# Layer 0 of a four-layer convolution kernel: group norm by half batches, a second channel tile taken from resident buffers, part of the statistics on ScalarE, another order of memory pools

## The chip, the cores and the metric

The kernel runs on one core of a Trainium2 chip. The core has five engines that run their own instruction streams and wait for one another by semaphores: TensorE (PE in the profile; PEld is its weight load), VectorE (DVE), ScalarE (ACT), GpSimd (POOL) and SyncE (SP). Transfers are issued from the queues of SP, ACT and POOL. The metric is the device time of one execution in microseconds (us). Three runs of the kernel before took 3128.01, 3133.1 and 3138.59 us, median 3133.1.

## The reference

The input `x` has shape (8, 384, 32, 32): eight images, 384 channels. Four layers follow one another, each `x = x + layer(group_norm(x))` with 32 groups of 12 channels. Layer 0 is the one that the change touches:

```python
def _bn(x, g, b):                       # mean and variance over all 8 images and all pixels
    m = x.mean(axis=(0, 2, 3), keepdims=True)
    v = x.var(axis=(0, 2, 3), keepdims=True)
    return (x - m) * lax.rsqrt(v + EPS) * g[None, :, None, None] + b[None, :, None, None]

def _dwproj(x, dw, g, b, pw):
    C = x.shape[1]
    y = lax.conv_general_dilated(x, dw, (1, 1), ((1, 1), (1, 1)), feature_group_count=C, ...)
    y = jax.nn.gelu(_bn(y, g, b), approximate=False)
    return jnp.einsum('oc,bchw->bohw', pw, y)

q = _dwproj(x, dw_q, g_q, b_q, pw_q).reshape(B, heads, hd, N)
k = _dwproj(x, dw_k, g_k, b_k, pw_k).reshape(B, heads, hd, N)
v = _dwproj(x, dw_v, g_v, b_v, pw_v).reshape(B, heads, hd, N)
attn = jax.nn.softmax(jnp.einsum('bhcn,bhcm->bhnm', q, k) * scale, axis=-1)
out = jnp.einsum('bhnm,bhcm->bhcn', attn, v).reshape(B, C, H, W)
out = jnp.einsum('oc,bchw->bohw', w_out, out)
return _bn(out, g_out, b_out)

def _gn(v, G=32, eps=1e-5):             # mean and variance of one image and one group
    g = v.reshape(B_, G, C_ // G, H_, W_)
    m = jnp.mean(g, axis=(2, 3, 4), keepdims=True)
    s = jnp.var(g, axis=(2, 3, 4), keepdims=True)
    return ((g - m) / jnp.sqrt(s + eps)).reshape(v.shape)
```

Two kinds of statistics matter. The group norm's are of one image each, so that four images can be normed before the other four are seen. The batch norm's (`_bn`) after each 3x3 depthwise convolution are of all eight images, so that the Gelu and the projections of q, k and v need all eight images of that convolution. Layers 1 to 3 (a mixture of experts, a 7x7 depthwise convolution, a branched mixer) come later in time and are not changed.

## The kernel before

The 384 channels lie as three channel tiles (`ct` 0 to 2) of 128 partitions; `VORDER = (1, 0, 2)` is the order k, q, v.

**Opening.** SP loads channel tiles 0 and 1 of all eight images into `x0` and `x1`. These two are the two buffers of the tag `o` in pool `co`; later the same buffers take the convolution's output. For each image and tile VectorE takes statistics (`x_stats`: two BATCH_NORM_STATS2 and an aggregate, L252 and L437). Then `gn_steps` (L259 to L300) norms all eight images of two channel tiles at once: TensorE averages over groups with small matmuls against `gmatA` (L279), VectorE forms centred moments (L290 to L293), TensorE averages these, VectorE adds epsilon (L246), POOL raises to the power -0.5 (`rsqrt`, L247), VectorE forms the offset (L297). `prepare0(0, b)` then applies scale and offset on ScalarE (`affine`, L354) and transposes 32x32 blocks on VectorE (L468) into `xt0`, which the convolution reads. Three parameter tensors (`bn_gb`, `bn_gbo`, `b2`) are loaded through ScalarE's queue.

**The loop.** The convolution runs as matmuls with banded weights. There are 36 groups, `groups = [(ct, v, u) ...]`: three channel tiles, three convolutions, four quarters `u` of the columns; four groups make one (ct, v). A group is 96 matmuls (L530) into one of two PSUM slots `ps`. Its other steps, in program order:

- `spread0(n + 2)` makes the matmul weights `wx` from loaded weights `w`, half on ScalarE (L486) and half on POOL (L487).
- `weights_of(n + 3)` issues the load of a later group's weights on ScalarE's queue (L478), three buffers.
- In groups 0 and 1, `stats2(b)` loads and measures channel tile 2 of four images each. After group 1 the norm of all three tiles and eight images begins, in a PSUM slot of its own between the groups (`slot0`); after group 2 it ends.
- `prepare0(1, b)` after groups 3, 4, 8, 9 and 10 loads channel tile 1 of each image again into a buffer `xn` (three buffers), norms and transposes it. `prepare0(2, b)` does the same for tile 2 in groups 12, 13, 16, 17 and 20.
- `results(ct, v, b, o)` for the four groups before: VectorE transposes an image's output back (L501), takes its batch norm statistics (L252, into `stats`), and SP stores it to `raw` (L503). The images go 1, 2, 2, 3 over the four groups; the last (ct, v) has its eight images after the loop.
- `evict_slots` copies the PSUM slot to `o` on ScalarE (L405). There are two `o` buffers: the first eviction of four groups needs the results of two sets before to be done.
- `coefs0(v)` turns the statistics of a finished convolution into a scale and an offset: three aggregates (L364), then L246, L247 and L367 to L369. It comes in groups 31 and 35 and after the loop. `gelu0` activates image 0 of k in groups 32 to 34, of q after the loop.

**After the loop.** `attention` loads `pw_v`, `w_out` (pool `aw`) and v of image 0 (`y`, pool `ay`) through SP, projects k and q of image 0 (L671), activates v and projects it (L726), and then runs attention image by image.

**What sets the order.** Within layer 0 the order on TensorE, ScalarE, VectorE and POOL is the order of the program text (`manual_schedule`); each engine takes its instructions strictly in order. SP's order, and POOL's in `attention`, is chosen by a planner. Pools lie on one stack of memory in the order in which they are opened: `cw` (statistics and parameters), `cxa` (`xt0`), `cy`, `co`. When they close, the pools of `attention` lie over the same addresses from the bottom, and what is written there waits for the last reader of what lay there. A DMA that is issued on SP's or ScalarE's queue can also wait for an earlier, unrelated DMA.

Of the kernel before, what the change touches and what calls it, by code (L numbers as in the profile page):

```python
# [18 lines left out]
P = 128  # L19
# [156 lines left out]
def conv_mixer_kernel(ctx: ExitStack, tc: tile.TileContext, a: dict, out: bass.AP):  # L176
# [82 lines left out]
    def gn_steps(mv, pool_ps, tag="gn", order="A"):  # L259
# [25 lines left out]
        def new(name):  # L285
            return small.tile(shape, FP, tag=f"gn_{name}{shape[1:]}", name=f"gn_{name}")
# [9 lines left out]
        rsqrt(flat(s), flat(pv))  # L296
        nc.vector.scalar_tensor_tensor(  # L297
# [114 lines left out]
    with (  # L412
        tc.tile_pool(name="cw", bufs=1) as cw,
        tc.tile_pool(name="cxa", bufs=1) as cxa,
        tc.tile_pool(name="cy", bufs=3, reuse_waits="tile") as cy,
        tc.tile_pool(name="co", bufs=2, reuse_waits="tile") as co,
        tc.manual_schedule(engines=ORDERED | {mybir.EngineType.Pool}),
    ):
        bn_gb = load(cw, "bn_gb", nc.scalar)
        bn_gbo, b2s = (load(cw, k, nc.scalar) for k in ("bn_gbo", "b2"))  # L420
# [7 lines left out]
        stats = cw.tile([P, 9, 2 * B, 6], FP, name="stats")  # L428

# [9 lines left out]

        with tc.tile_pool(name="cgn", bufs=2, space=PSUM) as cgn:  # L440
            pm = cgn.tile([P, NC, 2], FP, tag="gmy", name="pm", bufs=1)
            over_groups(pm, consts, range(NC))
            nc.scalar.copy(gmy, pm)
            for b in range(B):
                nc.sync.dma_start(out=x0[:, b], in_=a["x"][b, :, 0])
                nc.sync.dma_start(out=x1[:, b], in_=a["x"][b, :, 1])
                x_stats(0, b, x0[:, b])
                x_stats(1, b, x1[:, b])
            norms = {0: gn_coefs((mvx[:, 0, :2], mvx[:, 1, :2]), cgn)}

        with tc.tile_pool(name="cps", bufs=2, space=PSUM, reuse_waits="tile") as cps:
            xt0s = {}

            def prepare0(ct, b):

                if b == 0:
                    pool = cxb if ct == 1 else cxa
                    xt0s[ct] = pool.tile([P, 32, B, H + 2], FP, tag="xt0", name="xt0")
                    for row in (0, H + 1):
                        nc.gpsimd.memset(xt0s[ct][:, :, :, row : row + 1], 0.0)  # L460
                if ct == 0:
                    xn = x0[:, b]
                else:
                    xn = cy.tile([P, N], FP, tag="xn", name="xn")
                    nc.sync.dma_start(out=xn, in_=a["x"][b, :, ct, :])
                sx, tx = norms[ct]
                affine(xn, xn, sx[:, ct, b : b + 1], tx[:, ct, b : b + 1])
                nc.vector.transpose(  # L468
                    xt0s[ct][:, :, b, 1 : 1 + H].rearrange("p c h -> p h c"), img(xn)
                )  # L470

            groups = [(ct, v, u) for ct in range(NC) for v in VORDER for u in range(4)]
            weights0 = {}

            def weights_of(n):
                if n < len(groups):
                    w = cy.tile([P, 24, W], FP, tag="w", name="w")
                    nc.scalar.dma_start(out=w, in_=a["w0"][groups[n]])  # L478
                    weights0[n] = w

            def spread0(n):

                if n < len(groups):
                    w = weights0[n]
                    x = weights0[n] = cy.tile([P, 24, 2, W], FP, tag="wx", name="wx")
                    nc.scalar.activation(x[:, :, 0, :], w, AF.Copy, scale=parity[:, 0:1])  # L486
                    nc.gpsimd.tensor_scalar(x[:, :, 1, :], w, parity[:, 1:2], None, ALU.mult)  # L487

            def slot0():

                ps = cps.tile([P, 4, 2, B, H], FP, tag="ps", name="ps")
# [2080 lines left out]
```

## Time and profile before

| What | us |
|---|---|
| Median of three runs | 3133.1 |
| The profiled execution's own time | 3131.1 |
| Its span, first to last instruction | 3129.4 |
| First convolution matmul (L530) | 52.83 |
| First transposed result (L501) | 95.55 |
| Last convolution matmul ends | 274.2 |
| Last statistics of the last result end | 302.4 |
| First matmul on `pw_v` (L726) | 316.87 |
| Mean ACTIVATE of 128x1024 (L354, tile `y`) | 1.23 |
| Mean eviction of 128x2048 (L405, loop) | 1.86 |
| Power on POOL: 128x3, 128x16, 128x24 elements | 0.87, 2.94, 4.20 |

All times of the profile are of one execution, counted from its first instruction. A line of a timeline gives the start, the duration, the engine, the line of the kernel, the operation, what it writes and reads, how many instructions were merged, and in brackets the idle time of that engine before it with the releaser. A line of the stage table gives the length of the stage, each engine's busy time in it with the number of instructions, the granted clock of TensorE as a share of full speed, the busy share of the DMA engines and what they moved. A line of the waits gives the waiting engine and line, the one waited for, the total, the number of waits and the longest.

### The profile page before, as it was taken

The page shows a single profiled execution, that of the slowest core. Times are in us where ns is not written, and L with a number is a line of the kernel's source. Part 1 is how long each engine was busy: PE and PEld are TensorE (multiplying, and loading weights), DVE is VectorE, ACT ScalarE, POOL GpSimd, SP SyncE. Part 2 cuts the span into 40 slices and gives each one's busy share as a digit, 9 for nine tenths or more (in the row PEclk, how much of TensorE's full clock was granted, in tenths as well). Part 3 has the DMA queues.
Part 4 walks back from the last instruction along what each step waited for, and adds up shares of the span by engine and source line. Part 5 has one row for each costly group of instructions (what it writes and reads, how often), then busy time and mean ns, then how long its engine had stood idle before and what let it go on. Part 6 is the DMA issues. An engine that isn't in the chain of part 4 may idle for free. (4 is left out here: it accounts for less than half of the span.)

```text
span 3129.4 us, 45250 instructions
## 1 busy us (share of the span) xinstructions
PE 2978.0 (95%) x18280; PEld 1710.8 (55%) x18280; DVE 1857.4 (59%) x3066; ACT 1211.5 (39%) x1446; POOL 858.7 (27%) x1103
## 2 busy tenths in 40 slices
PE   4988999999999999999999999999999999886998
PEld 3765334343433434343433688788787877555543
DVE  6898344445454445444445777777777776457164
ACT  2655453544445353545433122222222223446520
POOL 2432000000000000000000577686777764111400
PEclk9999999999999999999999999999999999898999
DMA  6787102010111101110002111112112114967675
GB/s 220 262 281 287 57 23 83 23 63 23 61 46 41 63 23 63 44 63 23 31 23 94 74 41 65 57 49 85 45 45 81 52 37 161 335 204 251 232 227 187
DMA packets 89107, 323.03 MB, mean 103 GB/s; under 512 B 13608, under 2 KB 16000, under 8 KB 84664
## 3 DMA queue, kind: packets, MB, share of 16 engines
q1 hardware_dynamic: 64936, 251.71, 23.6%
q10 hardware_dynamic: 13776, 35.82, 3.7%
q0 software_dynamic: 10176, 32.51, 3.0%
q8 instruction: 146, 2.39, 0.3%
q14 instruction: 73, 0.60, 0.1%
HBM read 211.66 MB, written 111.68 MB: 103 GB/s over the span
## 5 line engine op out<-in xcount | busy, mean ns | idle before, releaser
L780 ACT ACTIVATE e<-sc 128x1024 f32<-128x1024 f32 x512 | 483.2, 1031 | 607.8 <-PE sc L773 607.7
L773 PE MATMUL sc<-qT,kT 64*128 64x512 f32 x2048 | 473.9, 602 | 0.0
L792 PE MATMUL av<-e,vT 128*64 128x512 f32 x2048 | 467.7, 599 | 0.0
L773 PEld LDWEIGHTS sc<-qT,kT 64*128 64x128 f32 x2048 | 186.8, 186 | 282.0 <-issue 231.3
L792 PEld LDWEIGHTS av<-e,vT 128*64 128x64 f32 x2048 | 135.5, 136 | 316.4 <-issue 316.4
L822 POOL DMA_DIRECT2D att<-att x45 | 23.7, 531 | 979.6 <-DVE att L817 979.6
L671 PE MATMUL sc<-y,pw 128*128 128x512 f32 x576 | 249.3, 594 | 0.0
L808 DVE LOAD_MASK_SELECT sm<-av x64 | 0.9, 14 | 417.0 <-PE av L792 417.0
L530 PE MATMUL ps<-xt,wx 64*64 64x256 f32 x3456 | 198.7, 388 | 35.2 <-DVE xt L468 20.1
L810 DVE RECIPROCAL inv<-sm 128x512 f32<-128x512 f32 x64 | 214.6, 3353 | 2.2
L1346 POOL TENSOR_TENSOR hs_sum<-hs,hs_sum 128x256 f32<-128x256 f32 (+1 forms) x225 | 209.7, 940 | 9.4
L1366 DVE TENSOR_TENSOR r<-r,p 128x256 f32<-128x256 f32 x416 | 153.2, 411 | 92.2 <-PE p L1357 90.7
L530 PEld LDWEIGHTS ps<-xt,wx 64*64 64x64 f32 x3456 | 156.8, 137 | 76.1 <-issue 39.7
L671 PEld LDWEIGHTS sc<-y,pw 128*128 128x128 f32 x576 | 108.8, 190 | 139.9 <-issue 138.5
L354 ACT ACTIVATE hs<-hs,b 128x512 f32<-128x512 f32 x135 | 88.4, 712 | 247.4 <-DVE hs L1308 246.8
L1116 PE MATMUL ps<-xt,wx 64*64 64x256 f32 (+1 forms) x2912 | 160.5, 379 | 23.8 <-ACT wx L1725 12.8
L1357 PE MATMUL p<-hs_sum,wsum 128*128 128x256 f32 x768 | 177.0, 384 | 0.0
L1308 DVE TENSOR_TENSOR hs<-p,hs_sum 128x256 f32<-128x256 f32 x270 | 114.5, 424 | 93.5 <-PE p L1299 39.0
L1299 PE MATMUL p<-forms,w 128*128 128x256 f32 x630 | 165.4, 379 | 0.0
L1323 PE MATMUL ph<-xn,w 128*128 128x512 f32 x342 | 159.3, 600 | 3.0 <-ACT xn L354 3.0
L1357 PEld LDWEIGHTS p<-hs_sum,wsum 128*128 128x128 f32 x768 | 149.2, 194 | 21.4
L1116 PEld LDWEIGHTS ps<-xt,wx 64*64 64x64 f32 x2912 | 109.2, 139 | 73.3 <-ACT wx L1725 15.1
(346 smaller groups left out, 4687.3 us busy)
## 6 DMA issues: line engine op xcount, KB each, us to landing
raw<-y SPq DMA_DIRECT2D x72, 512.0 KB
y<-raw SPq DMA_DIRECT2D x24, 1536.0 KB
x<-x SPq DMA_DIRECT2D x23, 608.0 KB
xt<-x SPq DMA_DIRECT2D x23, 608.0 KB
w<-in_w ACTq DMA_DIRECT2D x36, 384.0 KB
xn<-in_x SPq DMA_DIRECT2D x24, 512.0 KB
x<-in_x SPq DMA_DIRECT2D x16, 768.0 KB
z<-z POOLq DMA_DIRECT2D x16, 768.0 KB, 4.3
```

What stands on the lines that cost most here:

```text
L530: nc.tensor.matmul(ps[64 * d : 64 * d + 64, 2 * i + e, cc], lhsT=w[r, 12 * cc + 6 * e + 3 * d + k, :], rhs=xt0s[ct][r, 16 * d + 4 * u + 2 ...
L671: nc.tensor.matmul(ps[:, h, :], lhsT=w[:, ct, pair, :], rhs=y[:, ct, h * HF : (h + 1) * HF], start=ct == 0, stop=ct == NC - 1,)
L773: nc.tensor.matmul(sc[:, s, :], lhsT=kTs[b][r, pair, m * P : (m + 1) * P], rhs=qTs[b][r, pair, h * HF : (h + 1) * HF], start=True, stop=True,)
L780: nc.scalar.activation(e, sc, AF.Exp, scale=1.0 if shifted else HD**-0.5)
L792: nc.tensor.matmul(av[64 * s : 64 * s + 64, :], lhsT=vTs[0][:, m, c0 : c0 + 64], rhs=e[:, s, :], start=m == 0, stop=m == N // P - 1,)
L810: nc.vector.reciprocal(inv, sm)
L1116: nc.tensor.matmul(ps[64 * d : 64 * d + 64, 2 * i + e, c % 2, images], lhsT=w[r, d * K7 + k, :], rhs=by_slot(xts[ct])[r, 16 * d + column(c ...
L1299: nc.tensor.matmul(ps[:, :QF], lhsT=block1(PRODUCTS[n][0])[:, e], rhs=form_of(n, xn), start=True, stop=True,)
L1323: nc.tensor.matmul(ph, lhsT=w1[:, e, ct, dc * P : (dc + 1) * P], rhs=xn[:, ct, :], start=ct == 0, stop=ct == NC - 1,)
L1346: eng.tensor_add(rows_of(o, hs, s), rows_of(i, hs, s), rows_of(j, hs, s))
L1357: nc.tensor.matmul(ps[:, :QF], lhsT=block(w)[:, e], rhs=rows_of(x, hs, e), start=e == 0, stop=e == E - 1,)
L1366: nc.vector.tensor_tensor(out=o, in0=o, in1=ps[:, :QF], op=op)
```

## The change

1. **Opening.** The norm of tiles 0 and 1 is made in two halves of four images (`norm_steps`; `gn_steps` gets a pause before its last step, and tiles in pool `cw`). The first half's steps stand between the statistics of images 4 to 7; the second half's between the first transposes of `prepare0(0, b)`. The weights of groups 0 and 1 are loaded on SP's queue after image 3, and spread there; those of group 2 on ScalarE's queue later. The averaging of the constants (`pm`, `gmy`) moves behind the transposes. The three parameter loads go from ScalarE's queue to POOL's.
2. **Norm in the loop.** Also by halves. Each half's two passes over groups are put into the second halves of the PSUM slots of groups 2 and 3, between or ahead of these groups' own matmuls. `stats2` of images 4 to 7 is spread over groups 1 and 2. All eight images of tile 1 are prepared by group 4, in place from `x1`, with no second load.
3. **Statistics.** Of images 2 and 4, in all but the last (ct, v), VectorE takes no statistics. ScalarE makes two passes (`scalar_sums`, Identity and Square with an accumulated sum, against the channel's first mean as reference), after the group's eviction. `coefs0` first turns these sums into entries of the form that the aggregate reads (five more VectorE operations).
4. **Pools and queues.** `cw` is opened last. `pw_v` and v of image 0 are loaded through POOL's queue.

```diff
+        if pause:
+            yield
         nc.vector.scalar_tensor_tensor(
...
-        tc.tile_pool(name="cw", bufs=1) as cw,
         tc.tile_pool(name="cxa", bufs=1) as cxa,
         tc.tile_pool(name="cy", bufs=3, reuse_waits="tile") as cy,
         tc.tile_pool(name="co", bufs=2, reuse_waits="tile") as co,
+        tc.tile_pool(name="cw", bufs=1) as cw,
...
-        bn_gb = load(cw, "bn_gb", nc.scalar)
-        bn_gbo, b2s = (load(cw, k, nc.scalar) for k in ("bn_gbo", "b2"))
+        bn_gb, bn_gbo, b2s = (load(cw, k, nc.gpsimd) for k in ("bn_gb", "bn_gbo", "b2"))
...
+        def by_scalar(i):
+            v = stats[:, i].rearrange("p c a (s k) -> p c (a s) k", k=3)
+            return v[:, :, 8:24].rearrange("p c (j r) k -> p c j r k", j=2)[:, :, :, :4]
...
+        def prepare0(ct, b):
+            if ct < 2:
+                xn = (x0, x1)[ct][:, b]
+            else:
+                if b == 0:
+                    room0(ct)
+                xn = cy.tile([P, N], FP, tag="xn", name="xn")
+                nc.sync.dma_start(out=xn, in_=a["x"][b, :, ct, :])
+            sx, tx = norms[ct, b // HB]
+            q = b % HB
+            affine(xn, xn, sx[:, ct, q : q + 1], tx[:, ct, q : q + 1])
+            nc.vector.transpose(
+                xt0s[ct][:, :, b, 1 : 1 + H].rearrange("p c h -> p h c"), img(xn)
+            )
+
+        def norm_steps(nct, half, pool):
+            images = slice(HB * half, HB * half + HB)
+            return gn_steps((mvx[:, 0, :nct, images], mvx[:, 1, :nct, images]), pool, pause=True, own=cw)
+
+        room0(0)
         with tc.tile_pool(name="cgn", bufs=2, space=PSUM) as cgn:
+            for b in range(B):
+                nc.sync.dma_start(out=x0[:, b], in_=a["x"][b, :, 0])
+                nc.sync.dma_start(out=x1[:, b], in_=a["x"][b, :, 1])
+                if b == 3:
+                    for n in range(2):
+                        weights_of(n, nc.sync)
+                x_stats(0, b, x0[:, b])
+                x_stats(1, b, x1[:, b])
+                if b == 3:
+                    spread0(0)
+                if b == 4:
+                    norm = norm_steps(2, 0, cgn)
+                    next(norm)
+                if b == 5:
+                    next(norm)
+                    spread0(1)
+                if b == 6:
+                    norms[0, 0] = next(norm)
+            norm = norm_steps(2, 1, cgn)
+            for b in range(HB):
+                prepare0(0, b)
+                if b < 2:
+                    next(norm)
+                if b == 2:
+                    norms[0, 1] = next(norm)
+            weights_of(2)
+            for b in range(HB, B):
+                prepare0(0, b)
             pm = cgn.tile([P, NC, 2], FP, tag="gmy", name="pm", bufs=1)
             over_groups(pm, consts, range(NC))
             nc.scalar.copy(gmy, pm)
...
+            def scalar_sums(ct, v, j, y):
+                i = v * NC + ct
+                rest = cy.tile([P, N], FP, tag="xn", name="rest")
+                for k, func in enumerate((AF.Identity, AF.Square)):
+                    nc.scalar.activation(
+                        rest, y, func, bias=stats[:, i, 0, 1:2], scale=-1.0,
+                        accum_out=sums0[:, i, j, k : k + 1],
+                    )
...
             for n, (ct, v, u) in enumerate(groups):
...
+                ps, following = following or new_slots(), None
+                if n == 1:
+                    stats2(4)
+                    stats2(5)
+                if n == 2:
+                    go_on(0, ps)
+                    stats2(7)
+                    norms[1, 0] = norms[2, 0] = next(steps0[0])
+                if n == 3:
+                    prepare0(1, 1)
+                    go_on(1, ps)
+                    prepare0(1, 2)
+                    prepare0(1, 3)
+                    norms[1, 1] = norms[2, 1] = next(steps0[1])
                 for cc in range(2):
+                    if cc and n in (1, 2):
+                        following = new_slots()
+                        if n == 2:
+                            prepare0(1, 0)
+                        start_norm(n - 1, following)
+                        if n == 1:
+                            stats2(6)
...
-                for b in {3: (0, 1), 4: (2, 3), 8: (4, 5), 9: (6,), 10: (7,)}.get(n, ()):
-                    prepare0(1, b)
+                if n == 4:
+                    for b in range(HB, B):
+                        prepare0(1, b)
...
+                summed = None
                 if m > 0:
                     for b in ((0,), (1, 2), (3, 4), (5, 6, 7))[u]:
-                        results(*last, b, last_o)
+                        y = results(*last, b, last_o, b in (2, 4))
+                        if b in (2, 4):
+                            summed = (*last, b // 2 - 1, y)
...
                 evict_slots(o, ps, u)
+                if summed:
+                    scalar_sums(*summed)
...
-                pw_v = load(aw, "pw_v")
+                pw_v = load(aw, "pw_v", nc.gpsimd)
...
-                        nc.sync.dma_start(out=y, in_=raw[v][b])
+                        queue = nc.gpsimd if b == 0 and v == 2 else nc.sync
+                        queue.dma_start(out=y, in_=raw[v][b])
```

## The prediction

> **What bounds the kernel now.** I read the stages first, then VectorE's and TensorE's order of instructions, then the waits. The stages, cut where the work changes hands:
>
> ```profile
> core 0: us, PE busy (x) PEld busy (x) DVE busy (x) ACT busy (x) POOL busy (x), PEclk, DMA share, GB/s
> 0.00:52.83 52.83, 15.15 (x58) 13.36 (x59) 37.44 (x63) 17.18 (x27) 16.84 (x37) 1.00 0.60 228
> 95.55:302.40 206.85, 191.32 (x2989) 143.18 (x2982) 201.12 (x244) 114.16 (x89) 64.48 (x32) 0.98 0.82 285
> 302.40:316.87 14.47, 3.21 (x8) 1.14 (x7) 8.46 (x13) 3.41 (x4) 6.20 (x13) 0.77 0.96 364
> 316.87:3129.00 2812.13, 2728.98 (x14666) 1523.11 (x14666) 1589.70 (x2715) 1059.34 (x1314) 754.27 (x1012) 0.98 0.26 85
> ```
>
> The page's 95% TensorE is an average. In the opening (to 52.83) TensorE has nothing to do. From 95.55 to 302.40 VectorE is busy 201.12 of 206.85 us and is the bound. After 316.87 TensorE is; the change touches nothing there, so what is won or lost before 316.87 should reach the end. VectorE's order:
>
> ```profile
> 27.98 1.29 DVE L252 BATCH_NORM_STATS2 xst<-o 128x6 f32<-128x512 f32 x2 [2.28 <-DMA o<-in_x]
> 37.12 0.18 DVE L297 SCALAR_TENSOR_TENSOR gn_t<-gn_m,gn_s 128x16 f32<-128x16 f32 x1 [3.05 <-POOL gn_s L247]
> 38.61 14.08 DVE L468 STREAM_TRANSPOSE xt<-o 128x1024 f32<-128x1024 f32 x8 [1.31 <-ACT o L354]
> ...
> 95.55 1.21 DVE L501 STREAM_TRANSPOSE y<-o 128x1024 f32<-128x1024 f32 x1
> 96.80 1.29 DVE L252 BATCH_NORM_STATS2 stats<-y 128x6 f32<-128x512 f32 x2
> ```
>
> After the last image it idles through the norm until 38.61; each convolved image then costs a transpose (1.23) and its statistics (1.23). TensorE's bursts:
>
> ```profile
> 52.83 13.00 PE L530 MATMUL ps<-xt,wx 64*64 64x256 f32 x192 [18.97 <-DVE xt L468]
> ...
> 80.43 48.54 PE L530 MATMUL ps<-xt,wx 64*64 64x256 f32 x864 [0.37 <-DVE ve L246]
> 130.09 10.95 PE L530 MATMUL ps<-xt,wx 64*64 64x256 f32 x192 [1.13 <-DVE xt L468]
> 142.96 15.77 PE L530 MATMUL ps<-xt,wx 64*64 64x256 f32 x288 [1.92 <-ACT o L405]
> ...
> 168.09 23.75 PE L530 MATMUL ps<-xt,wx 64*64 64x256 f32 x384 [3.71 <-ACT o L405]
> ```
>
> A group of 96 matmuls takes 48.54/9 = 5.4. Groups 0 to 35 run from 52.83 to 274.2: 36 x 5.4 = 194.4 and 27.0 lost. 11.4 are lost before group 3 at 80.43 (cold clock 2.2, the norm inside the loop 9.2), 1.1 by 130.09, 14.5 in the last 24 groups. The waits say on what:
>
> ```profile
> ACT wx L486 <- DMA w<-in_w: 32.1, 15, 4.8
> ACT o L405 <- DVE y L501: 14.3, 5, 4.3
> ACT o L405 <- DMA raw<-y: 8.4, 3, 3.8
> ```
>
> ScalarE's eviction waits for VectorE to finish with the old `o` buffer. Call four groups a round, 0 to 8: TensorE pays 1.92 + 3.71 + 1.25 + 2.01 = 8.9 near the starts of rounds (142.96, 168.09, 193.09, 216.43). The other 5.6 are transfers that hold ScalarE and slow matmuls after 168.09.
>
> **How the parts add up.** The first matmul on `pw_v` (L726, at 316.87) waits for two paths, both counted from the last convolution matmul (274.2). TensorE itself still does the q and k projections, 274.4 to 305.6: +31.4. VectorE's path is the last eviction (+2.2), eight results (8 x 2.47 = 19.75), then 302.40 to 316.87 without the 6.02 that ScalarE waits for `y<-raw` (8.45): +30.4; with the 1.0 of new small operations (below) +31.4. So, with no lag, L726 starts at conv end + 31.4; now it starts 11.2 later (VectorE begins the last eight results 6.2 after the last eviction, the load costs 6.0, less the 1.0 not yet there). Gain = 11.2 + (274.2 - new conv end).
>
> **Opening.** With half the images normed while the other half load, the wait from 29.5 to 38.61 goes. VectorE does the same 16 statistics (1.4 each from 4.5) plus twelve small operations of 0.17. The two weight tiles on SP's queue ahead of image 4 add 0.79 MB, 2 us at the 400 GB/s of 10 to 20 us; three parameter loads leave ScalarE's queue for POOL's, behind the 448 KB `gmem` store (landing 7.4 after 12.79). POOL must then do consts (0.75), two memsets (1.3), one spread (2.2) and the power (16 elements 2.94, 24 elements 4.20: estimate 1.7 for 8). Loads down near 21.5 (20.2 and their own 1.3), that ends near 27.5. VectorE wants the scale at 25.0 (4.5, fourteen statistics, five small ones) and is held 2.5; all statistics end near 30.4. Eight transposes (14.08) and the second half's seven small operations (1.2), whose TensorE and POOL steps lie behind transposes, give a first convolution matmul at 46.0. Bounds: 44.5 without POOL's hold, 48 if the load ends 3 later; 46, since the POOL rows are direct. The moved constants' matmuls (3.14) and `gmy` copy lie under the transposes.
>
> **Norm in the loop.** It removes two passes (14 tiny matmuls each, about 2 us) and adds four of the same length. Following the order from 46.0: group 1's middle pass waits for `stats2` of images 0 to 3 (four at 1.4, the fourth load 3.9 after its buffer frees), hidden. The second pass ends at 62.9, power (estimate 2.3) and scale by 65.8; image 0's affine and transpose (1.23 + 1.9) end at 69. Group 3's second half waits for VectorE to read the variance behind image 1's transpose, ends at 79.1; its eviction 81. Scales for images 4 to 7 come at 80.4; their affines queue behind that eviction and a spread, their transposes end at 90.7. Eviction 4 needs that buffer (x1 sits in it), so group 6 starts at 92.7: 46.7 for six groups, 14.3 lost (bounds 10.2, passes and cold clock alone; 19, with 5 more of such queueing). What is bought: all eight images of the second tile are ready, VectorE turns to results at 90.7 not 95.55, and eight loads of 512 KB are gone from SP. The `xstmem` store (0.64 on POOL) moves to after group 3, behind nothing that is due.
>
> Every pass could also slow the clock. After the pass at 78.33 to 80.43 the windows from 82 to 86 show a granted clock of 0.50 and 0.73, worth 1.5 us; four such are 6 us. The order above holds 1 us of it (half groups of 3.2 and not 2.7). The Trainium skill, "TensorE: Matmul & The Clock Gate", Part 1, speaks against only longer pauses: the clock halves after an idle window of about 3.4 us. By the page four passes of 2 us cost nothing, and the sum would be 1 us less. By the row it would be 5 us more, which the bound of 19 covers; I stay with 1, because VectorE's transposes, not TensorE, set group 6.
>
> **Statistics moved.** 8 of 9 rounds x 2 images x 1.23 = 19.7 leave VectorE. Three `coefs0` calls add five operations of about 0.2: 3.0, of which 1.0 on the last path. With the four transposes (7.5) that moved ahead, VectorE's round falls from 19.7 and what it prepares to 17.3, and 22.9 in the two rounds that prepare three images, against TensorE's 21.6. So VectorE stops being the bound; TensorE is next, with ScalarE close. ScalarE gains 32 passes of 1.23 (L354's row for this size) and an accumulator read each (row at L2179: 0.191): 45.4. Its round holds 4 x (1.87 + 0.94) + 5.7 = 16.9, with three affines 20.6. Behind a waiting sum stand the next spread, weight issue and eviction. In round 3 the sum of image 2 waits for VectorE until 16.0 after the round's start (results from 7.9, one more transpose between), and the eviction of group 2 ends at 21.7, just in time; round 4 starts 3.8 later on ScalarE, and its eviction ends at 25.3 where 21.6 was needed. I take 6 for rounds 3 to 5, keep the 5.6 of transfers, drop the 8.9: 12 lost (bounds 3.1, today's waits on ScalarE held by transfers alone; 20, today's 14.5 plus the 5.7 of one round's sums).
>
> Square might need another activation table. The loop has one load, 1.28 at 262.58 for the Gelu. The Trainium skill, "ScalarE: Activation LUTs", Table sets, says cheap functions are in every set but names no Square there; if it is in none of these, round 8 alternates and pays four more loads, an estimate of 5.1 on ScalarE; no row shows it, and the sum leaves it out.
>
> **Tail.** With the statistics pool last, `pw_v`, `w_out` and `y` no longer wait for `bn_t` (SP issues them at 305.67 to 306.53). `pw_v` and `y` go past SP's queue to POOL's: issues of about 0.76 (row L845) before the power, which is not due until then. The 6.02 goes.
>
> **Sum.** Conv end 46.0 + 194.4 + 14.3 + 12 = 266.7. Gain 11.2 + 7.5 = 18.7. The profiled execution took 3131.1 (span 3129.4 and 1.7 around it), 2.0 under the median of the three runs; 3131.1 - 18.7 = 3112.4, forecast 3112. All best bounds: 44.5 + 194.4 + 10.2 + 3.1 = 252.2, gain 33.2, 3098; all worst: 48 + 194.4 + 19 + 20 = 281.4, gain 4.0, 3127. Likeliest's own range 3104 to 3120.
>
> **Rivals.**
> - *ScalarE hides its sums* (loss 3.1, opening at 44.5): conv end 256.3, gain 29.1: 3102. For it: ScalarE is busy only 114 of 206.85. Against: in-order waits. 0.20.
> - *The front yields nothing*: the first matmul stays at 52, because parameter or weight loads are late on shared queues. Conv end 272.7, gain 12.7: 3118. For: POOL's chain has no slack. 0.14.
> - *Transfers become the bound.* From group 6 on, 64 stores, 30 weights, 8 images, `pw` and two `y` are 53.9 MB; at 285 GB/s that is 189 us, conv end 281.7, gain 3.7: 3127, no change. Against: single windows of 10 us reach 320 to 336. 0.13.
> - *ScalarE's sums make it slower.* Each of two sums a round holds the next weight issue until its 4.5 us landing lies open: 16.9 + 9 = 26, 4.4 over TensorE's, x 8 = 35, plus eight affines (9.8): loss 45, conv end 299.7, gain -14.3: 3145. It decides from a loss of 31, 3.8 a round. For: 32.1 us of such waits now. Against: weights are asked for one group ahead. 0.09.
>
> **How the numbers follow.** Likeliest 0.40; the remaining 0.04 is shared out. A change of 0.3% (9.4 us) is about what a measurement of this kernel can tell from none: faster is below 3123.7, slower above 3142.5. Faster 0.40 + 0.20 + 0.14 + 0.03 = 0.77, same 0.13 + 0.01 = 0.14, slower 0.09. From 3098 to 3130 leaves out the slower case and the far end of the best.
>
> **What would show it.** Right: first L530 matmul (by the new lines) near 46; group 6 near 93; VectorE with idle time between 95 and 260; last convolution matmul near 267; no wait of the first v-Gelu on `y<-raw`; first `pw_v` matmul near 298. Wrong: waits of TensorE on evictions over 31 us in rounds 1 to 8; table loads beside Square; a first matmul after 50; a DMA share near 1 through the loop.

## The result, and the profile after

The changed kernel takes 3140.5 us (median of 20 runs) against 3132.1 for the kernel before (20 runs): ratio 1.0028, 95% interval 1.0021 to 1.0034. It is slower by 8.4 us, and 28.5 us above the forecast of 3112, outside its range. By the prediction's own limit of 0.3% (9.4 us) it is no change, to which it gave 0.14, where it gave 0.77 to faster. The profiled execution took 3140.7 us (span 3139.0).

The stages after, cut where the work changes hands (columns as in the stages of before: start and end, length, busy time of each engine, granted clock, DMA share, GB/s):

```profile
core 0: us, PE busy (x) PEld busy (x) DVE busy (x) ACT busy (x) POOL busy (x), PEclk, DMA share, GB/s
0.00:47.31 47.31, 18.83 (x75) 16.93 (x75) 38.91 (x69) 16.96 (x27) 19.99 (x44) 1.00 0.66 254
95.54:314.11 218.57, 193.26 (x2943) 139.74 (x2944) 175.83 (x218) 151.20 (x152) 66.94 (x44) 0.95 0.76 270
314.11:328.80 14.69, 4.10 (x10) 1.52 (x9) 9.07 (x18) 1.40 (x3) 4.99 (x3) 0.74 0.91 365
328.80:3139.00 2810.20, 2728.34 (x14666) 1523.26 (x14666) 1588.52 (x2715) 1059.10 (x1314) 753.33 (x1012) 0.98 0.26 85
```

VectorE is no longer full in the loop: 175.83 busy of 218.57, where it was 201.12 of 206.85. Yet the loop is 11.7 longer. The work after the first matmul on `pw_v` (now L825) is as long as before to 2 us, so the loss lies ahead of it. TensorE's bursts (start, length, last the wait in front and what ended it):

```profile
47.31 10.03 PE L626 MATMUL ps<-xt,wx 64*64 64x256 f32 x144 [8.18 <-DVE xt L484]
...
70.91 1.73 PE L279 MATMUL ps<-gn_d,gmatA 128*128 128x4 f32 x14
76.17 18.72 PE L626 MATMUL ps<-xt,wx 64*64 64x256 f32 x288 [3.54 <-DVE ve L246]
97.81 41.67 PE L626 MATMUL ps<-xt,wx 64*64 64x256 f32 x768 [2.91 <-ACT o L408]
144.13 12.01 PE L626 MATMUL ps<-xt,wx 64*64 64x256 f32 x192 [4.66 <-ACT o L408]
...
173.30 12.77 PE L626 MATMUL ps<-xt,wx 64*64 64x256 f32 x192 [4.91 <-ACT o L408]
...
202.53 34.23 PE L626 MATMUL ps<-xt,wx 64*64 64x256 f32 x576 [5.47 <-ACT o L408]
...
328.80 1.65 PE L825 MATMUL sc<-pw_v,y 128*128 128x384 f32 x2 [10.59 <-ACT y L357]
```

The first matmul came 5.5 earlier than before. Then three waits of about 5 us stand near the starts of rounds 3, 4 and 5 (ahead of groups 14, 18 and 22), with slow bursts behind them (12.01 and 12.77 for two groups that take 10.59 at full clock). The convolution ends at 281.2, and 47.6 us pass until L825, where it was 42.7. Where the time went:

| stretch | before | predicted | after |
|---|---|---|---|
| to the first convolution matmul | 52.8 | 46.0 | 47.3 |
| groups 0 to 5 | 43.8 | 46.7 | 50.5 |
| groups 6 to 35 | 177.6 | 174.0 | 183.4 |
| last convolution matmul to the first on `pw_v` | 42.7 | 31.4 | 47.6 |
| sum: first matmul on `pw_v` | 316.9 | 298.1 | 328.8 |

The end of the convolution is read here from the start of TensorE's projections. In the kernel before that is 274.4; with the 274.2 used above, its third row is 0.2 short and its fourth 0.2 long.

ScalarE's and VectorE's waits between 40 and 330 us (waiting engine, for what: us in all, times, longest):

```profile
DVE y L538 <- DMA raw<-y: 17.1, 9, 4.0
ACT rest L549 <- DVE y L538: 15.8, 5, 4.4
...
ACT y L357 <- DMA y<-raw: 13.3, 1, 13.3
...
ACT xn L357 <- DMA xn<-in_x: 8.0, 5, 4.2
ACT xn L357 <- DMA w<-in_w: 4.7, 1, 4.7
```

Three of these waits are new. VectorE waits for `y` buffers, where the kernel before shows

```profile
DVE y L501 <- DMA raw<-y: 1.0, 1, 1.0
```

The v-Gelu waits 13.3 for its load (6.0 before). ScalarE waits for the images of tile 2 (`xn`), whose affines stand ahead of the evictions that TensorE needs. SP's issues show why (start, length from the first to the last of a row's issues, count):

```profile
96.79 35.80 SPq L541 DMA_DIRECT2D raw<-y  x16
132.69 1.87 SPq L480 DMA_DIRECT2D xn<-in_x  x3
145.29 18.06 SPq L541 DMA_DIRECT2D raw<-y  x8
163.44 1.82 SPq L480 DMA_DIRECT2D xn<-in_x  x3
174.47 16.66 SPq L541 DMA_DIRECT2D raw<-y  x8
191.22 1.21 SPq L480 DMA_DIRECT2D xn<-in_x  x2
```

Each round's images are asked for only behind all eight result stores of the round before. In the kernel before they went out in ones and twos between the stores, from 117 to 169 us, as here in its round 4:

```profile
144.08 2.14 SPq L465 DMA_DIRECT2D xn<-in_x  x2
146.95 0.33 SPq L503 DMA_DIRECT2D raw<-y  x1
150.18 0.33 SPq L465 DMA_DIRECT2D xn<-in_x  x1
151.23 15.11 SPq L503 DMA_DIRECT2D raw<-y  x7
```

The scratch tile `rest` of `scalar_sums` carries the tag `xn`: twice a round it takes a place in the ring of three buffers that the image loads use.

### The profile page after: what moved, and what is told of

It reads as the page before. It is cut to its first block, busy times and chain, and to the rows that moved or that the text cites. A ratio compares the mean times of both kernels' runs of the same rounds, so it can differ in the third digit from the quotient of the medians.

```text
span 3139.0 us, 45387 instructions
## 1 busy us (share of the span) xinstructions
PE 2988.2 (95%) x18324; PEld 1713.1 (55%) x18324; DVE 1839.5 (59%) x3062; ACT 1248.6 (40%) x1510; POOL 861.4 (27%) x1111
```

## First experiments: one edit each

The theories: (1) the ring holds the image loads; (2) the sums themselves hold the evictions; (3) the v load stands behind POOL's power; (4) VectorE reads a variance too late in group 3. Each run was timed beside runs of the kernel before, whose medians were 3131.0 to 3131.9; in brackets behind a median stand its ratio to them and the 95% interval of that.

**A scratch of its own.**

```diff
-                rest = cy.tile([P, N], FP, tag="xn", name="rest")
+                rest = cy.tile([P, N], mybir.dt.bfloat16, tag="rest", name="rest", bufs=1)
```

> The scratch that ScalarE's sums write gets a buffer of its own (16-bit, since only 3 KB are left), in place of the ring of three xn buffers that the image loads of the third tile use. Theory 1, the ring: the loads can be issued ahead of the result stores again, the waits of the affines on them go, and TensorE's three stalls at the starts of rounds 3, 4 and 5 (4.66 + 4.91 + 5.47 us, and 5 us of cold clock behind them) shrink to the 2 to 4 us that they had in the kernel before. Last convolution matmul 266 to 270 instead of 281.2, time 10 to 15 us less than the changed kernel. Theory 2, the sums themselves hold the evictions, since each waits on ScalarE for VectorE's transpose: stalls stay within 1.5 us of what they are, last convolution matmul 278 or later, time within 3 us.

Measured: 3126.9 (0.9989, 0.9981 to 0.9998), 13.6 less than the changed kernel. SP's issues of this run:

```profile
96.52 34.70 SPq L541 DMA_DIRECT2D raw<-y  x16
137.17 2.12 SPq L480 DMA_DIRECT2D xn<-in_x  x2
140.03 0.33 SPq L541 DMA_DIRECT2D raw<-y  x1
```

The first three images now go before the row at 96.52, and the rows at 137.17 are the next round's. The waits on `xn<-in_x` are gone, the three stalls became 1.96, 3.15 and 1.42, and the convolution ends at 270.8. Theory 1 holds, theory 2 does not explain these stalls. The loss after group 6 (162 is 30 groups of 5.4) is 270.8 - 97.5 - 162 = 11.3, where I had predicted 12.

**The v load on SP's queue.**

```diff
-                        queue = nc.gpsimd if b == 0 and v == 2 else nc.sync
-                        queue.dma_start(out=y, in_=raw[v][b])
+                        nc.sync.dma_start(out=y, in_=raw[v][b])
```

> The load of the first image's v input goes back to SP's queue. Theory 3, POOL's order: on POOL it stood behind the power of the last coefficients (issued 317.46, 0.85 after the power); on SP it can go behind the last store, near 314.5, lands 9 to 10 later, and the first matmul on pw_v comes at 325 to 326 instead of 328.8: 3 us less. Rival, its buffer is the limit: it waits for something that ends with the last statistics or coefficients anyway, it is issued at 317 or later and the first matmul on pw_v stays within 1 us of 328.8, time within 1 us.

Measured: 3135.7 (1.0015, 1.0007 to 1.0024), 4.8 less than the changed kernel. In the changed kernel POOL issued the load 0.85 behind the start of the last coefficients' power, and ScalarE waited:

```profile
316.61 0.89 POOL L247 TENSOR_TENSOR bn_s<-ve,mhalf 128x3 f32<-128x3 f32 x1 [19.69 <-DVE ve L246]
317.46 0.61 POOL L752 DMA_DIRECT2D y<-raw  x1
...
327.51 3.50 ACT L357 ACTIVATE y<-y,bn_t,bn_s 128x1024 f32<-128x1024 f32 x3 [13.29 <-DMA y<-raw]
```

On SP it was issued behind the last store:

```profile
307.59 2.79 SPq L541 DMA_DIRECT2D raw<-y  x2
310.42 0.70 SPq L751 DMA_DIRECT2D y<-raw  x1
...
320.09 3.50 ACT L357 ACTIVATE y<-y,bn_t,bn_s 128x1024 f32<-128x1024 f32 x3 [8.53 <-DMA y<-raw]
```

From the end of the convolution to the first matmul on `pw_v` it is 43.5 (321.38 - 277.85), 4.1 less. Its buffer was not the limit; theory 3 holds. This run's convolution also ended 3.3 earlier than the changed kernel's with the same code there: that much the stalls vary from one execution to the next.

**The variance first.**

```diff
                 if n == 3:
-                    prepare0(1, 1)
                     go_on(1, ps)
+                    prepare0(1, 1)
```

> In group 3, VectorE reads the variance of the second half ahead of image 1's transpose, not behind it. Theory 4, VectorE's order of work: TensorE's wait of 3.54 us in the middle of group 3 goes (0 to 0.5 left), with it some of the slow clock after it, the scales of images 4 to 7 come 3 to 5 us sooner, and group 6 starts at 93 to 94.5 instead of 97.81; time 3 to 5 us less. Rival, the evictions' order on ScalarE sets it (the affines of images 4 to 7 stand behind the eviction of group 3 and a spread): group 6 stays within 1.5 us of 97.8, time within 1.5 us.

Measured: 3136.1 (1.0020, 1.0009 to 1.0030), 4.4 less. TensorE's bursts of this run:

```profile
73.98 17.46 PE L626 MATMUL ps<-xt,wx 64*64 64x256 f32 x288 [0.35 <-DVE ve L246]
94.45 43.36 PE L626 MATMUL ps<-xt,wx 64*64 64x256 f32 x768 [3.02 <-ACT o L408]
```

The wait of 3.54 fell to 0.35, and group 6 starts at 94.5. Theory 4 holds. It rests on the trace more than on the time, since this interval touches that of the changed kernel (1.0021 to 1.0034).

**No sums on ScalarE.** All images' statistics are VectorE's again, and the five small operations of `coefs0` are gone; everything else of the change stays.

```diff
-                        y = results(*last, b, last_o, b in (2, 4))
-                        if b in (2, 4):
-                            summed = (*last, b // 2 - 1, y)
+                        y = results(*last, b, last_o)
```

> All eight images' statistics on VectorE again; the rest of the change stays. Theory 1 (ring) and theory 2 (sums) both have the image loads ahead of the stores again, and the three stalls shrink to 2 to 4 us each. As my prediction's step on the moved statistics has it, VectorE is then the bound again: lag of 9 us at the starts of rounds and 6 us behind the last eviction, so it is 8 to 13 us slower than the kernel with the sums and the scratch of its own, and about level with the changed kernel (within 4). Theory 2 has it as fast as that kernel or faster, since the sums cost ScalarE more than they spare VectorE.

Measured: 3123.8 (0.9977, 0.9968 to 0.9986): 16.7 less than the changed kernel and 3.1 less than the one whose sums have their own scratch. My prediction's step, which had it 8 to 13 slower than that one, falls. The loss after group 6 is 268.4 - 98.3 - 162 = 8.1 without any sums, where it was 15.6 before. So the rest of the change takes about half of the loss out of the rounds by itself. I put it down to the eight images prepared ahead and their eight loads spared; no run takes these apart from the rest. VectorE's wait for `y` buffers, from the waits of this run, and then of the run with its own scratch:

```profile
DVE y L538 <- DMA raw<-y: 2.6, 2, 1.3
```

```profile
DVE y L538 <- DMA raw<-y: 17.0, 12, 5.0
```

The sums spare VectorE 16 x 1.23 less 3.0 = 16.7 net, and it waits 14.4 longer for buffers whose stores have not landed.

## The tail, and the edits together

**The v load on ScalarE's queue.**

```diff
-                        queue = nc.gpsimd if b == 0 and v == 2 else nc.sync
+                        queue = nc.scalar if b == 0 and v == 2 else nc.sync
```

> The changed kernel with the load of the first image's v input on ScalarE's queue, where it stands behind the three Gelus of k (done at 298), and its one store (image 0's last channels) has landed by then. Theory 3, the queue: nothing but its place behind POOL's power held it. It lands near 308, the last coefficients (318.1) become what the v-Gelu waits for, and the first matmul on pw_v comes at 319 to 321 instead of 328.8; time 8 to 10 us less. Rival, given back: an earlier load takes bandwidth from the last stores and the second image's loads, so that VectorE's last results or image 1 come later by what is won; time less by under 4.

Measured: 3130.7 (1.0001, 0.9991 to 1.0011), 9.8 less than the changed kernel, as theory 3 has it. The first matmul on `pw_v` is at 324.0, not 319 to 321:

```profile
302.48 1.02 ACT L357 ACTIVATE kT<-sc 128x1024 f32<-128x1024 f32 x1 [3.28 <-DMA raw<-y]
...
305.61 18.52 PE L770 MATMUL sc<-y,pw 128*128 128x512 f32 x36 [6.50 <-ACT kT L790]
```

The issue waits on ScalarE until its store has landed, the evictions of k queue behind it, and TensorE's own q and k projections end at 324.1. The load no longer sets the end, the projections do. At this matmul the profiled run is only 4.8 ahead of the changed kernel's; the other 3.9 by which these two differ (3131.9 against 3140.7) come after it, in work that no edit touches.

**The tail alone, on the kernel before.** The statistics pool goes last, `pw_v` to POOL's queue and v to ScalarE's, and nothing else changes.

```diff
-        tc.tile_pool(name="cw", bufs=1) as cw,
         tc.tile_pool(name="cxa", bufs=1) as cxa,
...
+        tc.tile_pool(name="cw", bufs=1) as cw,
...
-                pw_v = load(aw, "pw_v")
+                pw_v = load(aw, "pw_v", nc.gpsimd)
...
-                        nc.sync.dma_start(out=y, in_=raw[v][b])
+                        queue = nc.scalar if b == 0 and v == 2 else nc.sync
+                        queue.dma_start(out=y, in_=raw[v][b])
```

> The kernel before, with only the tail of the change and the v load on ScalarE's queue: statistics pool last, pw_v on POOL. My prediction's step: the 6.02 that the v-Gelu waits for its load goes, and no more, since ScalarE itself is free at 309.6: first matmul on pw_v at 310 to 312 instead of 316.87, time 5 to 7 us less than before. Rival: the tail's order cannot pay, because the load only takes its time elsewhere; time within 2 us of before.

Measured: 3117.7 (0.9955, 0.9938 to 0.9971), 13.3 under the kernel before. That is more than the 5 to 7 expected. The profiled run, the slowest of its six (3125.4), shows a tail of 35.7 (313.0 - 277.3) where it was 42.7, with the v-Gelu right behind ScalarE's own work. Its convolution ends 3 later, though, so that its first matmul on `pw_v` comes only 3.9 earlier. Where the other runs won the rest no profile shows.

**The three edits without sums.**

> The three edits together on the kernel without ScalarE's sums: no sums, the variance read first in group 3, v's load on ScalarE's queue. If the single edits add up: 3123.8 - 4.4 (variance first) - 11 (313.86 in the run without sums, against its coefficients at 301.1 and 1.3 more) = 3108, and 3104 to 3113 with what the parts share. If the transfers hold the last rounds whatever the order before them, the 4.4 are lost again at the stalls after 180 us: 3113 to 3117.

Measured: 3107.7 (0.9924, 0.9907 to 0.9942). The parts add. The profile has group 6 at 91.5, the end of the convolution at 263.1 and the first matmul on `pw_v` at 295.3: a tail of 32.2, where I had predicted 31.4.

**The three edits with sums.**

> ScalarE's sums with a scratch of their own, the variance read first in group 3, v's load on ScalarE's queue. If the single edits add up: 3126.9 - 4.4 - 10.5 (317.5 in the run with its own scratch, against its coefficients at 305.67 and 1.3 more) = 3112, and 3108 to 3117. My prediction, that the sums take the bound from VectorE, has it 8 us or more under the kernel without sums once nothing else holds the tail; the theory that they only move the work has it level or up to 6 us over.

Measured: 3113.7 (0.9943, 0.9927 to 0.9959). The parts add here too (13.6 + 9.8 + 4.4 = 27.8 off 3140.5 gives 3112.7). It is 6.0 above the kernel without sums. The two intervals overlap, but every run with sums (3111.5 to 3121.7) lies above every run without (3104.1 to 3109.2), so the sums cost, even with a scratch of their own.

**The front alone.** Norms by halves with the variance first, no sums, the pool and the tail's queues as before:

```diff
+        tc.tile_pool(name="cw", bufs=1) as cw,
         tc.tile_pool(name="cxa", bufs=1) as cxa,
...
-        tc.tile_pool(name="cw", bufs=1) as cw,
...
-                pw_v = load(aw, "pw_v", nc.gpsimd)
+                pw_v = load(aw, "pw_v")
...
-                        queue = nc.scalar if b == 0 and v == 2 else nc.sync
-                        queue.dma_start(out=y, in_=raw[v][b])
+                        nc.sync.dma_start(out=y, in_=raw[v][b])
```

> The front of the change alone: the norms four images at a time, with the variance read first in group 3, all statistics on VectorE, and the tail as it was before (statistics pool ahead of the others, the loads of pw_v and of v on SP's queue). If the parts add, it is the run of the three edits less the tail: 3107.7 + 13.3 = 3121, 8 to 12 us under the kernel before, with a tail of 42 to 45 us from the last convolution matmul to the first on pw_v. The rival that the front yields nothing, or is given back at the transfers of the last rounds: within 3 us of before.

Measured: 3122.7 (0.9969, 0.9958 to 0.9980), 9.2 under the kernel before; its tail is 42.7 (310.3 - 267.6). The sum holds, but not where I had looked for it: the first convolution matmul comes at 51.7, only 1.1 earlier than before, and the gain lies after group 6 (a loss of 267.6 - 96.7 - 162 = 8.9 against 15.6). POOL's and VectorE's rows of the opening:

```profile
20.30 0.56 POOL L377 DMA_DIRECT2D bn_gb<-in_bn_gb  x1 [6.76 <-DMA gmem<-gmatB]
...
32.52 0.88 DVE L300 SCALAR_TENSOR_TENSOR gn_t<-gn_m,gn_s 128x8 f32<-128x8 f32 x1 [5.81 <-POOL gn_s L247]
```

With the statistics pool in its old place the parameter loads wait for the `gmem` store, and POOL reaches the power 4.5 later. In the changed kernel they went out ahead of that store:

```profile
2.77 0.69 POOL L377 DMA_DIRECT2D bn_gb<-in_bn_gb  x1
...
28.02 0.88 DVE L300 SCALAR_TENSOR_TENSOR gn_t<-gn_m,gn_s 128x8 f32<-128x8 f32 x1 [1.17 <-POOL gn_s L247]
```

So, with these loads on POOL's queue, "statistics pool last" is worth 4.7 us in the opening (51.7 against 47.0 in the kernel with the three edits), and not in the tail alone.

## Why the sums cost

What was left: VectorE waits for stores because of the order of SP's queue, because all transfers share the DMA engines, or because of ScalarE's order.

**The two loads off SP's queue.** In the kernels with and without sums, the first image's q and k inputs (1.5 MB each) are loaded on POOL's queue, one group later.

```diff
-                if ct == NC - 1 and m % 3 and u == 1:
+                if ct == NC - 1 and m % 3 and u == 2:
                     y0 = pp0.tile([P, NC, N], FP, tag=f"y{before}", name="y0")
-                    nc.sync.dma_start(out=y0, in_=raw[before][0])
+                    nc.gpsimd.dma_start(out=y0, in_=raw[before][0])
```

> The kernel with the sums, their own scratch, the variance first and v's load on ScalarE's queue, and the two 1.5 MB loads of the first image's q and k inputs moved from SP's queue, where result stores stand behind them, to POOL's and one group later. If those loads make VectorE wait for y buffers (4.15 us at 272.26, just ahead of the last results), this wait goes, the last coefficients come 3 to 4 us sooner and the time falls by 3 to 5 us. If the sum of the transfers makes the stores late, whatever queue they are on: within 1.5 us.

> The same move of the two loads on the kernel without sums. VectorE waits for y buffers there by only 2.6 us in the whole loop, so little is to be had: within 2 us of 3107.7. If ScalarE's waits for transfers in the last rounds (evictions behind raw stores and the y load, some 10 us in all) come from that queue, 3 to 5 us less.

Measured: with sums 3113.7 (0.9940, 0.9923 to 0.9956), no change; VectorE's waits for buffers are 18.5 where they were 19.8. It is not the queue of these loads. The Trainium skill, "DMA: Bandwidth & Descriptors", Issuing engines are not separate DMA queues, says the same: transfers from any engine run on the same 16 DMA engines, and another queue saves only the time to issue. Without sums: 3103.2 (0.9908, 0.9893 to 0.9924), 4.5 under the run before it; these intervals overlap, and its first matmul on `pw_v` is no earlier (298.1), so I don't take this gain as shown. In the profiles of this pair the cost of the sums lies behind the convolution: with them it ends at 263.7, without at 267.0, yet VectorE begins the last eight results at 277.5 with them and at 270.7 without.

**Without the weights' transfers.** Only the first three groups' weights are loaded and used again for all 36.

```diff
-                w = cy.tile([P, 24, W], FP, tag="w", name="w")
-                queue.dma_start(out=w, in_=a["w0"][groups[n]])
-                weights0[n] = w
+                if n < 3:
+                    w = cy.tile([P, 24, W], FP, tag="w", name="w")
+                    queue.dma_start(out=w, in_=a["w0"][groups[n]])
+                    kept.append(w)
+                weights0[n] = kept[n % 3]
```

> The kernel without sums, with the variance first and v's load on ScalarE's queue, in which only the first three groups' weights are loaded and then used again for all 36 (the convolution of layer 0 is left without its other weights): 33 transfers of 0.39 MB fewer in the loop, the engines' work the same. If transfers hold the last rounds (DMA share 0.91 from 200 to 250 us, ScalarE waiting for weights 25 us), TensorE's 9.6 us of stalls after group 6 fall under 4 and the time is 5 to 8 us less. If VectorE's pace holds them (busy 48 to 50 of 50 us), the stalls stay within 2.5 us of 9.6.

> The kernel with ScalarE's sums, their own scratch, the variance first and v's load on ScalarE's queue, again with only the first three groups' weights loaded (33 transfers of 0.39 MB fewer, the convolution of layer 0 without its other weights). With the sums VectorE waits 17 to 20 us for y buffers whose stores have not landed, against 0 to 3 without them. If the share of the DMA engines is what makes those stores late, these waits fall under 8 us and the time to 5 to 9 us under that of the same kernel with its weights (3113.7), at or under the one without sums (3107.7). If it is the order on ScalarE, whose sums wait for VectorE and hold evictions, the time stays within 3 us of 3113.7 whatever the waits for buffers do.

Measured (medians; intervals 0.9914 to 0.9945 and 0.9889 to 0.9924 in the right column):

| | all weights loaded | three groups' weights loaded |
|---|---|---|
| VectorE takes all statistics | 3107.7 | 3109.5 |
| ScalarE takes two of eight | 3113.7 | 3101.9 |

Without sums, no gain shows: a quarter of the loop's bytes fewer, and the time is the same within its interval. VectorE holds that kernel: it is as busy with fewer transfers as with all, and begins its last eight results no sooner (271.6 against 269.5). The stages with all weights (columns as above):

```profile
97.00:150.00 53.00, 53.00 (x988) 44.68 (x984) 52.34 (x61) 31.22 (x24) 22.27 (x12) 1.00 0.83 294
150.00:200.00 50.00, 46.39 (x829) 38.49 (x825) 49.41 (x57) 26.86 (x21) 18.48 (x9) 0.97 0.75 257
```

and with three groups' weights:

```profile
97.00:150.00 53.00, 53.00 (x988) 44.70 (x984) 52.34 (x62) 31.93 (x25) 23.06 (x12) 1.00 0.59 226
150.00:200.00 50.00, 46.48 (x864) 38.81 (x859) 49.41 (x56) 25.51 (x20) 19.83 (x9) 1.00 0.50 194
```

TensorE is full up to 150 too. Its stalls after group 6 are 10.0 (9.6 with all weights), but 4.1 of them are a new wait for POOL.

With sums, the transfers are what holds: with a quarter of them taken away, 11.8 us go, more than the 5 to 9 expected. VectorE's waits for buffers fall to 8.8, a little over the 8 expected:

```profile
DVE y L538 <- DMA raw<-y: 19.8, 11, 6.6
```

```profile
DVE y L540 <- DMA raw<-y: 8.8, 4, 3.7
```

and TensorE has one stall left after group 6:

```profile
93.93 74.78 PE L628 MATMUL ps<-xt,wx 64*64 64x256 f32 x1344 [3.00 <-ACT o L408]
171.47 84.80 PE L628 MATMUL ps<-xt,wx 64*64 64x256 f32 x1536 [2.76 <-ACT o L408]
```

There the sums do about what they were predicted to: 7.6 us less than without. In the real kernel the bound passes from VectorE to the transfers before that is won. Part of the 11.8 could be ScalarE's own waits for weights (24.8 us before this edit), which go with the same transfers; these runs don't part the two.

## Why the prediction was wrong, step by step

- **Opening: right in its sum, in part by luck.** 47.3 against 46.0, inside 44.5 to 48. The parameter loads did not go behind the `gmem` store, so POOL held VectorE 1.17 and not 2.5; but VectorE wanted the scale only at 26.9 and not at 25.0, 1.37 of it a wait for an image. The run of the front alone shows what the order that I had assumed costs: 51.7, a hold of 5.81, and not 46.
- **Norm in the loop: too good by 3.8, inside its bounds.** Group 6 at 97.8 against 92.7. I had let VectorE read the variance behind image 1's transpose without pricing the wait, and that transpose itself waited 3.9 for an affine that stood behind eviction 2. I had only group 3's second half stand behind this read; in the trace all its matmuls do (the pass at 70.91, then 3.54 of waiting). Reading it first gives 3.4 back. The slow clock is the rest: I took 1 us, and the three groups after the last pass took 18.72 where 15.77 is full speed.
- **Groups 6 to 35: too good by 9.4, over its bound.** The failed step is "Statistics moved". It priced ScalarE's passes, their order and their waits, but not the tile that they write. That tile takes places in the ring of the image loads, and SP's in-order queue then puts these loads behind eight stores. I had counted "eight loads gone" and never asked when the other eight go. With its own scratch the loss is 11.3, the 12 of the prediction.
- **The same step's drop of 8.9 was right in size, but not by its cause.** About half of the loss goes without any sums (15.6 to 8.1): the stalls of rounds 3 and 4 (1.92 and 3.71 before) are gone, those from 186.62 on, 3.49 the first, stay. The sums cost 6 us in the kernel with all three edits. The third rival (transfers become the bound) came nearest to the mechanism: DMA share 0.76 over the loop did not rule it out, since a store that lands late holds one of four buffers. That its end of the convolution, 281.7, nearly meets the measured 281.2 is luck: with a scratch of its own and the same transfers it is 270.8.
- **Tail: too good by 16.2, and I gave it no bound of its own.** "The 6.02 goes" failed. I wrote that POOL would issue the v load before the power. It came behind it, landed 10.0 us later, and ScalarE waited 13.3 for it. Of the 16.2, 5.2 are this: 14.69 from the end of the last statistics to the first matmul on `pw_v`, where I had 9.45. The other 11.0 are VectorE's start on the last eight results, 13.2 after the convolution's end where I took 2.2 and "no lag". When the convolution ended, VectorE still had one wait for a buffer (3.9, to 285.51), two images of the old round (5.0) and the coefficients of q (3.9) ahead of it. From the end of the convolution to this start it is 10.7 to 13.9 in all kernels with ScalarE's sums and 3.7 to 9.9 in those without, so it does not come from a full VectorE alone, as I had put it.
- **The tail of 31.4 itself can be had:** 32.2 in the run without sums, with the load on ScalarE's queue.
- **Square's table: no cost.** One table load stands in the loop, at 268.52, for the Gelu, as before. No run shows a load beside a Square.
- **ScalarE's sums make it slower**, the rival on this side of no change, put the price at 45 lost in evictions that wait for sums and weights. The loss was 21.4 and mostly by other waits; that the sums do cost, by 6 us and late stores, is not what it said.
- **None of the four signs of being wrong came true:** TensorE waited 22.0 for evictions, no table was loaded for Square, the first matmul came at 47.3, and the DMA share was 0.76. None of them looked at the scratch, at POOL's order or at the tail.

The three oversights are 13.6 + 9.8 + 4.4 = 27.8 us, and the forecast missed by 28.5; with all three edits the change takes 3113.7. That this meets the 3112 so nearly is in part luck. The tail is still 39.9 in the profile of that kernel (its slowest run) and 40.6 in that of the one with the two loads moved (3114.4), not 31.4. In the second, groups 0 to 35 took 216.6 where I had 220.7, and the work after the first matmul on `pw_v` was 4 us shorter than before; both hide the long tail, which no edit with sums took away.

## A version that beats both

The change without its third part, with the variance read first and v's load on ScalarE's queue: 3107.7, ratio to the kernel before 0.9924 (0.9907 to 0.9942), 23.3 us faster than before and 32.8 faster than the change. Moving the two early loads to POOL's queue as well gave 3103.2 (0.9908, 0.9893 to 0.9924).

## What to carry to other kernels

Ask of every tile that a change adds which ring it takes a place in and who else waits for that ring, even if nobody reads the tile: a scratch cost more here (13.6) than the passes that wrote it (6.0). A transfer moved to another queue goes where that queue's order puts it, so find the instruction in front of it and ask what that one waits for. Work taken off a full engine is won only up to the next resource, and a mean share of it (0.76 here) doesn't show whether its single transfers still land in time.

## What the runs showed of the hardware

- An ACTIVATE with an accumulated sum over 128x1024 took 1.15 and a separate read of the accumulator 0.19; with 16-bit output the ACTIVATE was again 1.15.
- TensorE's clock fell after shorter pauses than I had thought. In the changed kernel, 4.66 of waiting was followed by windows with a granted clock of 0.50. In the run with the v load on ScalarE's queue a pause of 2.60 had 0.50 from 158 to 160, and in the run with its own scratch a pause of 3.15 had 1.00 throughout. In the run with the v load on SP's queue, pauses of 2.62 and 2.63 were followed by 12.28 and 10.59 us for two groups. The Trainium skill, "TensorE: Matmul & The Clock Gate", Part 1, puts the fall at an idle window of about 3.4 us that runs free of the kernel. A free window explains that equal pauses end differently; a fall after 2.60, shorter than the window, it does not explain.
- Three kernels with the same code up to the end of the convolution ended it at 277.8, 281.2 and 281.7 in their profiles. From the first matmul on `pw_v` to the end, work that no edit touches, the profiles of all kernels here took between 2803.5 and 2813.0. An edit worth a few us has to be priced from medians, and what one profile shows of it read stage by stage.
